# Order of the jobs beside attention, and the border of a local attention as one product, in a fused two-layer kernel on one Trainium2 core

## The chip, the cores and the metric

The kernel runs on one core of a Trainium2 chip. Its engines work side by side, each through its own list of instructions in order: TensorE (PE, matrix products), VectorE (DVE), ScalarE (ACT), GpSimd (POOL), and SyncE (SP), which here only issues transfers. They wait for each other by semaphores. The metric is the device time of one execution in microseconds (us), lower is better.

## The reference

Input and output are four images of 64 x 64 positions with 256 channels, float32. Two layers follow one another.

```python
# layer 0: attention over all 4096 positions of an image
q, k, v = x @ Wq + bq, x @ Wk + bk, x @ Wv + bv          # q, k: 32 channels
x = gamma * (softmax(q @ k.T) @ v) + x
# layer 1: 3x3 depthwise convolution to 3 x 256 channels, two pointwise layers, residual
hid = gelu(w_up1 @ conv3x3(x) + b_up1)                   # 768 -> 512 channels
h = x + (w_up2 @ hid + b_up2)                            # 512 -> 256
# then attention of each position over its 3x3 neighbours, padded with zeros, residual
q, k, v = split(w_qkv @ h + b_qkv)
w = softmax over the 9 neighbours of (q . k) / 16
out = h + sum over the 9 neighbours of w * v
```

At the border of an image the missing neighbours have k = b_k, so their scores are not zero weights: the kernel adds exp of a score for them to the denominator.

## The kernel before, in words

Everything is in one function, `unshifted`, with its order written out by hand. An image is cut into 8 blocks of 8 rows (512 positions); the four images give 32 **slots**. In a slot, layer 0 attends with the 512 queries of one block. A slot has 16 **points** (8 groups of keys, two halves each). At a point PE multiplies weights by values (`product`, L308, tile `acc`, eight records, 3.4 us); at every even point it first makes the next energies (`energy`, L289, tile `e`); ACT turns these into weights `p` (`weight`, L297); DVE sums them up (`add_up`, L322, tile `den`).

Layer 1 fills the gaps between these products, some slots later. The list `jobs` gives each point its pieces for block k = slot - 3 and block a = slot - 5. In order:

- `hidden_part` (L527): the first pointwise layer for half of the channels (d) in two parts, with 7 quarter products by recombined weights in place of 8. Part 0 makes `hid_a`, which ACT copies out (L540), and `hid_bc`, which DVE adds out (L534); part 1 makes `hid_de` and `hid_gf`, which DVE adds out, and ACT applies gelu (L550).
- `update` (L584, tile `dx`): the second pointwise layer; DVE adds the residual and stores `h` (L590).
- `guide` (L670, tile `g`, read out by ACT into `lq`) and `scores` (L763, tile `s`): the scores of the local attention, against `wg`, the product of the query and key weights. ACT takes exp (L783, tile `lp`), POOL masks the neighbours.
- `local_values` (L722, tile `lv`): values of half a block; DVE adds the bias (L735).
- `border`: `wc` times the pixels at the left and right edge, and of the first or last row of an image; a product with one output row (L702, tile `c`) of 8 and 8, and at 8 of the 32 blocks also 64, columns. ACT takes exp into `pad` (L708), POOL scales it.
- `local_sum` on POOL adds `lp` and `pad` to the denominator; `local_total` (tile `ld`) sums it over the partitions by a product with `ones`, `local_reciprocal` inverts it on DVE; `local_product` (L853, tile `lo`) makes the output, which DVE scales (L860), and one of POOL and DVE adds to `h`; SP sends it to memory.

The 3x3 convolution (`perceive`, L463) runs on DVE, whose generator `conv` is advanced by a number of **steps** at each point: a step is a tap (one instruction) or a recombination (L469); the first tap of each output is ACT's (L459). `n_steps` sets the pace, `-(-(point + 1) * n_steps // (points - 2))` steps up to each point.

At the end of a slot `partial_sums` and `finish` follow: DVE sums `den`, PE adds it up over the partitions (L361, tile `dps`), DVE inverts it, scales `acc` (L373) and adds the result into the ring of rows `xp` (L378); `rim` then copies or clears a border row of the ring. `finish` runs between the last point of a slot and point 0 of the next.

[...] four for `e`, two for `acc`, and two, tag `m`, that all jobs and `dps` take by turns (`job_bank`). A job's first product waits until the job two places before it has been read out of its bank.

The order of the work before, at the places which the change touches: point 0 holds `local_values` of block k-1 (second half), then part 0 of the hidden layer; `border` of block k-1 runs at point 8 ahead of the energies; in the last slot (31) the next block's jobs are put in as well and a second convolution is chained to the first (`upper`, all outputs without the last row's last taps). After slot 31 a tail without layer 0 finishes blocks 29 to 31, with jobs and convolution steps in a list of their own; it has four more banks. `DIRECT` is 28: blocks from there on have their output made in the tail. The tile `o` (two buffers) holds both the results of `finish` and the outputs `lo`.

Of the kernel before, what the change touches and what calls it, by code (L numbers as in the profile page):

```python
# [9 lines left out]
F32 = mybir.dt.float32  # L10
# [5 lines left out]
P = 128  # L16
# [4 lines left out]
HP, WP = H + 2, W + 2  # L21
NB = 512
RB = NB // W
NBLK = N // NB
NT = N // P
TPB = NB // P
# [25 lines left out]
def attention_then_perception_kernel(  # L52
# [34 lines left out]
    def unshifted():  # L87
# [54 lines left out]
        for c in range(CH):  # L142
            nc.gpsimd.memset(xp[:, c, 0:WP], 0.0)
            nc.gpsimd.memset(xp[:, c, (RP - 1) * WP :], 0.0)


        near = pool.tile([P, 2, QR, QW], F32, tag="near", name="near")
# [431 lines left out]
        def update(s, c):  # L579
            if c == 0:  # L580
                below(s)
            ps = job_bank(f"dx_{s}_{c}")
            for d in range(NHC):
                nc.tensor.matmul(  # L584
                    ps, lhsT=wup2[:, d, bass.ts(c, P)], rhs=hids[s][:, d, :],
                    start=(d == 0), stop=(d == NHC - 1),
                )
            for half in range(2):
                cols = slice(half * KW, (half + 1) * KW)
                nc.vector.scalar_tensor_tensor(  # L590
                    hs[s][:, c, half, HALO:, :],
                    ps.rearrange("p (h w) -> p h w", w=W)[:, :, cols],
                    bup2[:, c : c + 1],
                    xv[:, c, ring(s) : ring(s) + RB, 1 + cols.start : 1 + cols.stop],
                    ALU.add, ALU.add,
                )

# [85 lines left out]
        def edge_row(s):  # L685
            return {0: 0, NBLK - 1: RB - 1}.get(s % NBLK)

        def border(s):


            ps = job_bank(f"c_{s}")
            row = edge_row(s)
            n_side = 2 * RB
            parts = [
                (slice(half * RB, (half + 1) * RB), lambda h, half=half: h[:, :, half, half * (KW - 1)])
                for half in range(2)
            ]
            if row is not None:
                parts.append((slice(n_side, n_side + W), lambda h: h[:, row]))
            for to, of in parts:  # L700
                for kin in range(CH):
                    nc.tensor.matmul(  # L702
                        ps[0:1, to], lhsT=wc[:, kin : kin + 1], rhs=of(pixels(s, kin)),
                        start=(kin == 0), stop=(kin == CH - 1),
                    )
            n = parts[-1][0].stop
            one = pad[0:1, :]
            nc.scalar.activation(one[:, :n], ps[0:1, :n], AF.Exp, bias=bc, scale=-(C**-0.5))  # L708
            nc.gpsimd.tensor_scalar(one[:, :n], one[:, :n], 3.0, None, ALU.mult)
            if row is not None:  # L710

                ends = one[:, n_side : n : W - 1]
                nc.gpsimd.tensor_scalar(ends, ends, 2.0 / 3.0, None, ALU.mult)
# [133 lines left out]
        def local_product(s, c):  # L847
            b, g = divmod(s, NBLK)
            ps = job_bank(f"lo_{s}_{c}")
            pv = ps.rearrange("p (h w) -> p h w", w=W)  # L850
            todo = [(half, *piece) for half in range(2) for piece in pieces(s)]
            for i, (half, (block, t), rows, of) in enumerate(todo):
                nc.tensor.matmul(  # L853
                    pv[:, rows, columns(half)],
                    lhsT=lvs[block, t, half][:, bass.ts(c, P)],
                    rhs=near_ws[block, half][:, t, of, :],
                    start=(i == 0), stop=(i == len(todo) - 1), skip_group_check=True,
                )
            o = tile_of([P, NB], "o", f"lo_{s}_{c}", 2)
            nc.vector.tensor_tensor(o, ps, lrdens[s], ALU.mult)  # L860
            if s < NSLOT - 1:
                watch(o)
            engine, res = nc.gpsimd, o
            if s >= DIRECT and s != NSLOT - 2:

                if c == 0:
                    results[s] = tile_of([P, CH, NB], "xc", f"res_{s}", 2)
                engine, res = nc.vector, results[s][:, c, :]
            ov, rv = (t.rearrange("p (h a w) -> p h a w", a=2, w=KW) for t in (o, res))
            engine.tensor_tensor(rv, ov, pixels(s, c), ALU.add)  # L870
            nc.sync.dma_start(out=out[b, :, c, bass.ts(g, NB)], in_=res)
# [36 lines left out]
        for slot in range(NSLOT):  # L908
            b, g = divmod(slot, NBLK)
            if slot >= RING:  # L910
# [1 line left out]
            k, a = slot - LAG_HID, slot - LAG_ATT  # L912

            jobs = [
                job(local_values, k - 1, 1) + job(hidden_part, k, 0, 0),
                job(local_denominator, a) + job(hidden_part, k, 0, 1),
                job(hidden_part, k, 1, 0), job(hidden_part, k, 1, 1),
                job(local_product, a, 0), job(local_product, a, 1),
                job(update, k, 0), job(update, k, 1), [],
                job(guide, k, 0), job(guide, k, 1), job(scores, k, 0),  # L920
                job(scores, k, 1) + job(local_sum, k - 1), job(local_values, k, 0), [], [],
            ]
            if slot in (1, 2):
                jobs[0] = [lambda: next(combine)] * 2
# [10 lines left out]
            if slot == NSLOT - 1:  # L935


                jobs = [
                    job(local_values, k - 1, 1) + job(hidden_part, k, 0, 0),
                    job(local_denominator, a) + job(hidden_part, k, 0, 1),  # L940
                    job(hidden_part, k, 1, 0), job(hidden_part, k, 1, 1) + job(local_product, a, 0),
                    job(update, k, 0), job(update, k, 1) + job(local_product, a, 1),
                    job(local_values, k, 0) + job(guide, k, 0),
                    job(local_values, k, 1) + job(guide, k, 1),
                    job(scores, k, 0) + job(hidden_part, k + 1, 0, 0),
                    job(scores, k, 1) + job(local_sum, k - 1) + job(hidden_part, k + 1, 0, 1),
                    job(local_total, a + 1) + job(local_reciprocal, a + 1)
                    + job(hidden_part, k + 1, 1, 0),
                    job(hidden_part, k + 1, 1, 1), job(update, k + 1, 0) + job(border, k),
                    job(local_product, a + 1, 0) + job(update, k + 1, 1),  # L950
                    job(local_product, a + 1, 1) + job(local_values, k + 1, 0),
                    job(local_values, k + 1, 1),
                ]
                conv = chain(conv, perceive(slot - 1, upper))
                n_steps += NPC * (TAPS - 1 + 3)
            for point in range(points):
                G, half = divmod(point, 2)
                after = slot + (G + 1) // NG, (G + 1) % NG
                if half == 0:
                    if G == NG // 2 and slot + 1 < NSLOT:  # L960
                        spread_queries(slot + 1)

                    if G == NG // 2:
                        for do in job(border, k - 1):
                            do()
                    if after[0] < NSLOT:
                        energy(*after)
                if after[0] < NSLOT:
                    weight(*after, half)
                for do in jobs[point]:  # L970
                    do()
                product(slot, G, half)

                if point == 0:
                    add_up(slot, 0, 0)
                if point < points - 1:
                    add_up(slot, *divmod(point + 1, 2))
                else:
                    partial_sums(slot)

                to = min(n_steps, -(-(point + 1) * n_steps // (points - 2)))
                if point < 3:

                    to = min(to, n_mixed // MULT)
                while stepped < to:
                    next(conv, None)
                    stepped += 1
                if slot == 0 and point == NG:

                    next(combine)  # L990
                    blqk = loaded(b_lqk, "blqk")
                    wperc = loaded(w_perc, "wperc")
                    bperc = loaded(b_perc, "bperc")
                    wup1 = loaded(w_up1, "wup1")
                    bup1 = loaded(b_up1, "bup1")
                    wup2 = loaded(w_up2, "wup2")
                    mix_weights()
                    bup2 = loaded(b_up2, "bup2")
                    nc.sync.dma_start(out=wlv, in_=w_qkv[:, :, 2 * C :])
                    blv = loaded(b_lv.partition_broadcast(P), "blv", [P, C])  # L1000
                if nxt and half == 1:
                    for do in nxt[G]:
                        do()
                    if slot and G + 2 < NBLK:
                        fetch(slot + 1 + G + 2)
# [465 lines left out]
```

## Time and profile before

| | |
|---|---|
| time, median of three runs | 3551.79 us (3550.02 to 3551.85) |
| span of the profiled execution | 3549.7 us |
| PE busy | 98% of the span |
| DVE busy | 69% |
| ACT busy | 31% |
| POOL busy | 18% |
| granted PE clock, mean | 0.998 |
| slot, from the start of one to the next | 104.9 us |
| slot 31 (3282.7 to 3428.3) | 145.6 us |
| tail (3428.3 to the end) | 121.4 us |

Busy time is the time in which an engine has an instruction running. PE's records of one line are given with their count: a float32 product shows as two records. A wait is idle time of an engine put down to what released it; "issue" means that nothing in the profile was waited for. A line of a timeline gives the start in us from the start of the span, the length in us, the engine, the line of the kernel, the operation and the tiles (written <- read), and in brackets the idle time ahead of it with its releaser. The ends of PE's records are modelled, so the distance from one start to the next is the better measure of what PE work costs.

### The profile page before, as it was taken

The page shows a single profiled execution, that of the slowest core. Times are in us where ns is not written, and L with a number is a line of the kernel's source. Part 1 is how long each engine was busy: PE and PEld are TensorE (multiplying, and loading weights), DVE is VectorE, ACT ScalarE, POOL GpSimd, SP SyncE. Part 2 cuts the span into 40 slices and gives each one's busy share as a digit, 9 for nine tenths or more (in the row PEclk, how much of TensorE's full clock was granted, in tenths as well). Part 3 has the DMA queues.
Part 4 walks back from the last instruction along what each step waited for, and adds up shares of the span by engine and source line. Part 5 has one row for each costly group of instructions (what it writes and reads, how often), then busy time and mean ns, then how long its engine had stood idle before and what let it go on. Part 6 is the DMA issues. An engine that isn't in the chain of part 4 may idle for free.

```text
span 3549.7 us, 32536 instructions
## 1 busy us (share of the span) xinstructions
PE 3483.7 (98%) x12426; PEld 1903.1 (54%) x12426; DVE 2463.6 (69%) x3471; ACT 1084.7 (31%) x1336; POOL 628.9 (18%) x815
## 2 busy tenths in 40 slices
PE   9999999999999999999999999999999999999998
PEld 4444555555555555565555555555555555555555
DVE  1386777657777777765777777776577777777975
ACT  3232332323332323332332323333323323223331
POOL 2000012111121221121111212111121122121223
PEclk9999999999999999999999999999999999999999
DMA  3000000120000000011000000001100000000000
GB/s 104 7 4 10 7 16 19 24 48 16 9 16 7 16 15 15 22 27 42 15 16 16 4 13 16 15 22 36 33 15 16 16 10 10 13 15 16 7 6 25
DMA packets 92997, 66.86 MB, mean 19 GB/s; under 512 B 65856, under 2 KB 70976, under 8 KB 92704
## 3 DMA queue, kind: packets, MB, share of 16 engines
q1 hardware_dynamic: 92160, 64.29, 6.6%
q8 instruction: 100, 1.64, 0.2%
q14 instruction: 65, 0.53, 0.0%
q10 hardware_dynamic: 672, 0.39, 0.0%
HBM read 43.49 MB, written 18.81 MB: 18 GB/s over the span
## 4 chain that ended last, share of the span: by engine, by line
PE 92%; DVE 6%; issue 1%; DMA 0%; SPq 0%; POOL 0%; ACT 0%; ACTq 0%; DVEq 0%; POOLq 0%
PE acc L308 49%; PE e L289 7%; PE dx L584 6%; PE hid_bc L527 5%; PE hid_de L527 4%; PE hid_gf L527 4%; PE g L670 3%; PE v L255 3%; PE lo L853 3%; PE s L763 2%; PE lv L722 2%; DVE xp L378 1%; DVE perc L463 1%; PE hid_a L527 1%; PE hid L559 1%; PE qk L221 1%
## 5 line engine op out<-in xcount | busy, mean ns | idle before, releaser
L308 PE MATMUL acc<-p,v 128*128 128x512 f32 x4096 | 1842.4, 595 | 0.2 <-DVE o L373 0.2
L308 PEld LDWEIGHTS acc<-p,v 128*128 128x128 f32 x4096 | 765.7, 190 | 885.1 <-issue 876.2
L463 DVE SCALAR_TENSOR_TENSOR perc<-xp,wperc,perc 128x512 f32<-128x512 f32 (+2 forms) x1554 | 1159.3, 805 | 64.9 <-ACT perc L459 64.9
L297 ACT ACTIVATE p<-e 128x1024 f32<-128x1024 f32 x512 | 523.8, 1023 | 1473.9 <-PE e L289 471.0
L322 DVE TENSOR_TENSOR den<-den,p 128x1024 f32<-128x1024 f32 x480 | 586.1, 1221 | 104.0 <-ACT p L297 102.3
L181 POOL TENSOR_TENSOR watched<-watched,lo 128x256 f32<-128x256 f32 x124 | 150.0, 1210 | 1070.5 <-DVE lo L860 1065.5
L289 PE MATMUL e<-qa,ka 32*128 32x512 f32 x2048 | 292.0, 640 | 0.0
L584 PE MATMUL dx<-hid,wup 128*128 128x512 f32 x512 | 233.0, 598 | 0.0
L787 POOL TENSOR_TENSOR lp<-lp,near 128x396 f32<-128x396 f32 x60 | 87.2, 1453 | 678.3 <-ACT lp L783 678.3
L534 DVE TENSOR_TENSOR hid<-hid_bc,hid 128x512 f32<-128x512 f32 x60 | 41.5, 691 | 219.9 <-PE hid_bc L527 219.9
L735 DVE TENSOR_TENSOR lv<-lv,blv 128x256 f32<-128x256 f32 x126 | 47.1, 414 | 188.3 <-PE lv L722 188.3
L469 DVE TENSOR_TENSOR perc<-perc 128x256 f32<-128x256 f32 x360 | 171.6, 490 | 7.2
L527 PE MATMUL hid_de<-perc,wmix 128*128 128x256 f32 x720 | 165.2, 379 | 0.0
L584 PEld LDWEIGHTS dx<-hid,wup 128*128 128x128 f32 x512 | 94.7, 190 | 129.9 <-issue 101.4
L527 PEld LDWEIGHTS hid_de<-perc,wmix 128*128 128x128 f32 x720 | 136.8, 190 | 43.7 <-issue 28.2
L289 PEld LDWEIGHTS e<-qa,ka 32*128 32x128 f32 x2048 | 79.9, 183 | 148.0 <-issue 145.0
L550 ACT ACTIVATE hid<-hid,bup 128x512 f32<-128x512 f32 x120 | 80.1, 714 | 215.8 <-DVE hid L534 215.8
L459 ACT ACTIVATE perc<-xp,bperc,wperc 128x512 f32<-128x512 f32 x192 | 145.2, 806 | 0.0
L590 DVE SCALAR_TENSOR_TENSOR h<-dx,bup,xp 128x256 f32<-128x256 f32 x128 | 56.0, 479 | 117.9 <-PE dx L584 117.9
L527 PE MATMUL hid_bc<-perc,wup 128*128 128x256 f32 x360 | 90.5, 387 | 41.3 <-DVE lv L735 38.5
L722 PE MATMUL lv<-wlv,h 128*128 128x256 f32 x520 | 126.5, 385 | 3.9 <-DVE lv L735 3.1
L722 PEld LDWEIGHTS lv<-wlv,h 128*128 128x128 f32 x520 | 96.1, 190 | 53.8 <-issue 35.2
(143 smaller groups left out, 2907.3 us busy)
## 6 DMA issues: line engine op xcount, KB each, us to landing
xp<-in_x SPq DMA_DIRECT2D x30, 528.0 KB, 4.0
out<-lo SPq DMA_DIRECT2D x58, 256.0 KB, 2.0
xc<-in_x SPq DMA_DIRECT2D x56, 256.0 KB, 3.8
qa<-packed SPq DMA_DIRECT2D x124, 64.0 KB, 2.0
ka<-st SPq DMA_DIRECT2D x124, 16.0 KB, 1.8
packed<-st SPq DMA_DIRECT2D x31, 64.0 KB, 1.9
wup<-in_w_up SPq DMA_DIRECT2D x1, 1536.0 KB, 6.9
out<-res SPq DMA_DIRECT2D x6, 256.0 KB, 2.0
```

Of the source, the lines that this page charges most:

```text
L181: nc.gpsimd.tensor_tensor(at, at, values[:, i : min(n, i + C)], ALU.add)
L255: nc.tensor.matmul(ps[:, i * C : (i + 1) * C], lhsT=xc[:, kin, bass.ts(2 * pair + i, P)], rhs=wv[:, kin, :], start=(kin == 0), stop=(kin = ...
L289: nc.tensor.matmul(e[:, j, :], lhsT=key[rows, :], rhs=queries[s][rows, :], start=True, stop=True,)
L297: nc.scalar.activation(p, energies[s, G][:, 2 * half : 2 * half + 2, :], AF.Exp)
L308: nc.tensor.matmul(accs[s][c], lhsT=v[:, 2 * half + i, bass.ts(c, P)], rhs=p[:, i, :], start=(first and i == 0), stop=(G == NG - 1 and hal ...
L322: nc.vector.tensor_tensor(den, den, p, ALU.add)
L459: nc.scalar.activation(acc, win, AF.Identity, bias=bperc[:, half, j : j + 1], scale=wt)
L463: nc.vector.scalar_tensor_tensor(acc, win, wt, acc, ALU.mult, ALU.add)
L469: nc.vector.tensor_tensor(t[:, to, :], t[:, a, :], t[:, b, :], op)
L527: nc.tensor.matmul(ps[:, n * C : (n + 1) * C], lhsT=w(j), rhs=mixes[s, j][:, kind, :], start=(j == 0), stop=(j == MULT - 1),)
L584: nc.tensor.matmul(ps, lhsT=wup2[:, d, bass.ts(c, P)], rhs=hids[s][:, d, :], start=(d == 0), stop=(d == NHC - 1),)
L722: nc.tensor.matmul(ps[:, half * C : (half + 1) * C], lhsT=keys_of(s, t, half, kin), rhs=wlv[:, kin, :], start=(kin == 0), stop=(kin == CH ...
```

## The change

Six edits:

1. At point 0 of every slot part 0 of the hidden layer is put ahead of `local_values`; in slot 31 the guides go ahead of the local values too, and a hidden part ahead of `local_total` and `local_reciprocal`.
2. `border` is one product: DVE makes the sum over the two channel halves of `h` times `wc` in a tile `edge` (`border_terms`, two small instructions for each part, at the end of `update`), and PE multiplies it by `ones`, so that every partition gets the sum.
3. `border` moves from point 8 of the following slot to point 14 of the block's own slot.
4. In slot 31 `n_steps` counts 48 steps of the chained convolution, which is what it yields, in place of 66.
5. The outputs `lo` of blocks from 28 on use a buffer of `p` (three buffers, which hold weights until then) in place of one of `o` (two).
6. Ten products of `ones` by `ones` (128 columns) stand at the start of PE's list.

```diff
+WARM = 10
...
+        warm = bank("m", "warm")
+        for _ in range(WARM):
+            nc.tensor.matmul(warm[:, :P], lhsT=ones, rhs=ones, start=True, stop=True)
...
+            if c == CH - 1:
+                border_terms(s)
...
+        def border_terms(s):
+            for to, of in border_parts(s):
+                nc.vector.tensor_scalar(edge[:, to], of(0), wc[:, 0:1], None, ALU.mult)
+                nc.vector.scalar_tensor_tensor(
+                    edge[:, to], of(1), wc[:, 1:2], edge[:, to], ALU.mult, ALU.add
+                )
...
-            for to, of in parts:
-                for kin in range(CH):
-                    nc.tensor.matmul(
-                        ps[0:1, to], lhsT=wc[:, kin : kin + 1], rhs=of(pixels(s, kin)),
-                        start=(kin == 0), stop=(kin == CH - 1),
-                    )
-            n = parts[-1][0].stop
+            n = border_parts(s)[-1][0].stop
+            nc.tensor.matmul(ps[:, :n], lhsT=ones, rhs=edge[:, :n], start=True, stop=True)
...
-            o = tile_of([P, NB], "o", f"lo_{s}_{c}", 2)
+            if s < DIRECT:
+                o = tile_of([P, NB], "o", f"lo_{s}_{c}", 2)
+            else:
+                o = tile_of([P, 2, NB], "p", f"lo_{s}_{c}", 3)[:, 0, :]
...
-                job(local_values, k - 1, 1) + job(hidden_part, k, 0, 0),
+                job(hidden_part, k, 0, 0) + job(local_values, k - 1, 1),
...
-                job(scores, k, 1) + job(local_sum, k - 1), job(local_values, k, 0), [], [],
+                job(scores, k, 1) + job(local_sum, k - 1), job(local_values, k, 0), job(border, k), [],
...
-                    job(local_values, k, 0) + job(guide, k, 0),
-                    job(local_values, k, 1) + job(guide, k, 1),
+                    job(guide, k, 0) + job(local_values, k, 0),
+                    job(guide, k, 1) + job(local_values, k, 1),
...
-                    job(local_total, a + 1) + job(local_reciprocal, a + 1)
-                    + job(hidden_part, k + 1, 1, 0),
+                    job(hidden_part, k + 1, 1, 0) + job(local_total, a + 1)
+                    + job(local_reciprocal, a + 1),
...
-                n_steps += NPC * (TAPS - 1 + 3)
+                n_steps += NPC * (TAPS - 1)
...
-                    if G == NG // 2:
-                        for do in job(border, k - 1):
-                            do()
```

In `border_parts` the left edge has columns 0 to 7 of `edge`, the right edge 8 to 15, and an edge row, at the first and last block of an image, 16 to 79 in two halves of 32.

More of the change, by code (lines that the diff above doesn't have):

```diff
@@ L686, in edge_row, with border_parts @@
             return {0: 0, NBLK - 1: RB - 1}.get(s % NBLK)
+        edge = pool.tile([P, 2 * RB + W], F32, tag="edge", name="edge")
+        def border_parts(s):
+            row = edge_row(s)
+            parts = [
+                (slice(half * RB, (half + 1) * RB), lambda c, half=half: hs[s][:, c, half, HALO:, half * (KW - 1)])
+                for half in range(2)
+            ]
+            if row is not None:
+                parts += [
+                    (
+                        slice(2 * RB + half * KW, 2 * RB + (half + 1) * KW),
+                        lambda c, half=half: hs[s][:, c, half, HALO + row, :],
+                    )
+                    for half in range(2)
+                ]
+            return parts
+        def border_terms(s):
[3 more added lines that the diff above has]
+                    edge[:, to], of(1), wc[:, 1:2], edge[:, to], ALU.mult, ALU.add
+                )
         def border(s):
@@ L693, in border @@
             n_side = 2 * RB
[L694 to L699, printed above, removed]
-            for to, of in parts:
-                for kin in range(CH):
-                    nc.tensor.matmul(
-                        ps[0:1, to], lhsT=wc[:, kin : kin + 1], rhs=of(pixels(s, kin)),
-                        start=(kin == 0), stop=(kin == CH - 1),
-                    )
-            n = parts[-1][0].stop
+            n = border_parts(s)[-1][0].stop
+            nc.tensor.matmul(ps[:, :n], lhsT=ones, rhs=edge[:, :n], start=True, stop=True)
             one = pad[0:1, :]
@@ L938, in unshifted @@
                 jobs = [
-                    job(local_values, k - 1, 1) + job(hidden_part, k, 0, 0),
+                    job(hidden_part, k, 0, 0) + job(local_values, k - 1, 1),
                     job(local_denominator, a) + job(hidden_part, k, 0, 1),
```

## The prediction

> **What bounds the kernel now.** I read the page first, then the list of waits of TensorE (PE), then the timelines of PE, VectorE (DVE) and ScalarE (ACT) around one slot boundary, around the last slot and at both ends.
>
> ```profile
> PE 3483.7 (98%) x12426; PEld 1903.1 (54%) x12426; DVE 2463.6 (69%) x3471; ACT 1084.7 (31%) x1336; POOL 628.9 (18%) x815
> PE hid_bc L527 <- DVE lv L735: 38.5, 28, 1.4
> PE lv L722 <- DVE lv L735: 3.1, 1, 3.1
> PE hid_bc L527 <- DVE lturned L841: 2.8, 1, 2.8
> ```
>
> PE is busy all but 66 us of 3549.7, and the chain that ended last is 92% PE. So only two things can move the time: PE work, and the waits of PE (columns: total us, times, longest). One wait is 38.5 us: `hid_bc`, once in each of slots 4 to 31, for VectorE to empty a bank of local values. The boundary from slot 11 to 12 (start, us, what):
>
> ```profile
> 1324.36 0.30 PE L361 MATMUL dps<-parts,fold 128*128 128x32 f32 x2
> 1325.66 1.99 PE L722 MATMUL lv<-wlv,h 128*128 128x256 f32 x8
> 1327.49 1.46 PE L527 MATMUL hid_a<-perc,wup 128*128 128x256 f32 x6
> 1330.32 1.56 PE L527 MATMUL hid_bc<-perc,wup 128*128 128x256 f32 x6 [1.37 <-DVE lv L735]
> ...
> 1327.62 1.98 DVE L378 SCALAR_TENSOR_TENSOR xp<-o,gbv,xp 128x512 f32<-128x512 f32 x2
> 1329.52 0.74 DVE L735 TENSOR_TENSOR lv<-lv,blv 128x256 f32<-128x256 f32 x2
> ...
> 1329.63 0.30 ACT L399 COPY xp<-xp 128x132 f32<-128x132 f32 x1 [7.49 <-DVE xp L378]
> 1330.76 0.36 ACT L540 COPY hid<-hid_a 128x256 f32<-128x256 f32 x1
> 1433.82 0.37 ACT L540 COPY hid<-hid_a 128x256 f32<-128x256 f32 x1 [2.17 <-PE hid_a L527]
> ```
>
> Two banks alternate. `lv` is done at 1327.5, but DVE finishes the old slot until 1329.6 and only then empties it; `hid_bc` needs that bank. The last two lines matter later: in slot 12 ACT is held by the copy of a border row, in slot 13 it waits for PE.
>
> [...] eight `qk` matmuls take 3.04 us at 9.16 and 1.94 us at 18.00. [...] at 1329.63 everything on ACT stands behind the row copy.
>
> **The change part by part**, against the profiled span of 3549.7 (the timed runs, 3550.0 to 3551.9, have a median 2.1 higher; I take the saving off that).
>
> *Hidden quarters ahead of local values (slots 4 to 31).* New order: `dps`, energies, `hid_a`, `hid_bc`, `lv`. With `border` now just before `dps`, `hid_a` gets border's bank, `hid_bc` that of `dps` (emptied by the reciprocal at 1325.06), `lv` that of `hid_a` (emptied by the ACT copy). On the timeline: energies end and `hid_a` starts at 1325.66, takes 1.40; `hid_bc` starts at 1327.06 with no wait, takes 2.6; `lv` may start at 1329.66. Where ACT is free, as in slot 13, the copy follows `hid_a` within 0.5 us, long before: nothing waits, 1.37 is saved. DVE adds `hid_bc` at about 1330.0 and `lv` at 1331.6, while PE multiplies 3.4 us of `acc`; `hid_de` and `hid_gf` come later than both. Where ACT copies a border row (g = 3 and 4, four images, so 8 boundaries: the waits list has 4 + 4 of these, 7.5 us each) the copy of `hid_a` ends at 1331.12, `lv` waits 1.5, and the gain is nil. Sum: 20 x 1.37 = 27.4, and 8 x 0 = 0.
>
> *Border as one product.* Before, eight records take 0.28 us start to start, twelve 0.51:
>
> ```profile
> 1388.62 0.35 PE L702 MATMUL c<-h,small 128*1 128x8 f32 x8
> 3528.78 0.59 PE L702 MATMUL c<-h,small 128*1 128x8 f32 x12
> 3452.36 0.32 PE L833 MATMUL ld<-pad,ones 128*128 128x16 f32 x2
> ```
>
> (The next PE instructions start at 1388.90, 3529.29 and 3452.60.) After, one product of `ones` with 16 columns, the form of the third row: 0.24. For the 80 columns of the eight blocks at an image edge I take 0.25, since `dps` with 32 columns takes 0.23 (1324.36 to 1324.59). Saved: 24 x 0.04 + 8 x 0.26 = 3.0 us; bounds 0 (each product exposes 0.1 more behind the energies, as `acc` does: 3.70 there, 3.60 elsewhere) and 5 (it hides beside its neighbours).
>
> *Border terms on DVE.* Four small instructions more for each block, eight at an image edge. No row has their shape; nearest are scalar_tensor_tensor 128x1 (158 ns) and 128x64 (278 ns): 0.2 each, 0.8 us, or 1.6. In a slot they stand behind `h`; queued behind them are one `den` sum and the convolution's taps; DVE then idles 6.08 us before the next `lv` at 1417.8, so they cost 0, both bounds. In the tail DVE is full from 3461.8 to 3484.6 and `ld` waits 1.25 for a DVE mask: 0.6 lost there (0 to 1.5).
>
> *Border's new place.* Its exp on ACT follows the `p` exp of 1317.60, so about 1318.7. It overwrites `pad`, which POOL's `local_sum` reads until 1313.5: 5 us of room. Behind it on ACT is only the next `p`, at 1321.1. POOL's own small product follows into 7.7 us of idleness. No DMA is issued or passed. Cost 0.
>
> *Last slot.* The phantom steps go (126 to 108), so DVE takes 7.7 taps a point instead of 9, and 11 instead of 16 at point 3.
>
> ```profile
> 3320.51 12.63 DVE L463 SCALAR_TENSOR_TENSOR perc<-xp,wperc,perc 128x512 f32<-128x512 f32 x16
> 3342.39 8.01 DVE L463 SCALAR_TENSOR_TENSOR perc<-xp,wperc,perc 128x512 f32<-128x512 f32 x9
> 3351.12 1.99 PE L722 MATMUL lv<-wlv,h 128*128 128x256 f32 x8 [3.11 <-DVE lv L735]
> ```
>
> The reader sees bursts of taps on DVE, and PE stopped behind them. The waits of PE in this slot, beside that of `hid_bc` for `lv`, are 3.11 + 2.81 + 0.52 + 0.38 = 6.8 (the last two for `h`). With 11 taps (8.7 us) `h` is out at 3328 rather than 3334; guide ahead of `lv` puts 1.7 us more before the second `lv`, which needs its bank at about 3347 while DVE has emptied it by 3344; `ld` after the quarters is read by DVE 6 us before its bank is wanted. The tight place is point 8: step 60 of the mixed convolution now comes at point 7, about 3355, and `hid_bc` of the next block wants it at 3356. The work taken out of the middle lands in 11.7 us of DVE idleness after 3404. I take 6.0 (2 to 6.8).
>
> *The start.* Ten warm-up products of 128 columns fill PE from 1.05 (its operand is set by then) to 5.47, where it waits for `wv`. Twenty records of 99 columns go at 0.13 each in `lo` (twelve in 1.54)[...]: they end by 6.3, no later than the second `v` product, which waits for ACT's copy until 6.30 anyway. That costs 0. [...] six `v` records go in 1.3 instead of 2.2 us and the `qk` in 1.9 instead of 3.0. Those 2.0 pass on down the chain: ACT's `st`, its four transfers and its copies (the rows they copy have landed by 11.66), `qk` at 18.00, then SP's `ka` from 20.71, which SP reaches with 2 us to spare. I take 2.0; bounds 0 [...] and 2.6 (the restart of `qk` too).
>
> *The end.* `lo` of the last blocks takes three buffers `p` instead of two `o`.
>
> ```profile
> 3538.59 0.69 DVE L860 TENSOR_TENSOR lo<-lo,lrden 128x512 f32<-128x512 f32 x1 [0.73 <-DMA out<-lo]
> 3541.18 0.69 DVE L860 TENSOR_TENSOR lo<-lo,lrden 128x512 f32<-128x512 f32 x1 [1.18 <-DMA out<-lo]
> ```
>
> The first could start at 3537.87, the second after two 0.7 us operations, at 3539.3, when the buffer three back is free: 1.9 earlier, and nothing ends later than that chain.
>
> Sum: 27.4 + 3.0 + 6.0 + 2.0 + 1.9 - 0.6 = 39.7, rounded to 40: span 3510, time 3512.
>
> **Rivals.** *A, the wait moves to ACT in every slot*, not in eight: then 27.4 is lost and 12.6 remain, 3539. For it: [...] the row copies show what it does. Against: ACT L540 waited for PE, not the reverse, in 22 cases (44.5 us). *B, the last slot stays bound by DVE* (121.4 us busy of 145.6): the 6.0 becomes 0, and the start gives 0 too: 3520. For it: the margin of 1 us at point 8. Against: 11.7 us of idle DVE in that slot. *C, slower*: as A, but ACT later still. Price: the wait of `lv` is the end of ACT's copy less 1329.7, in 28 slots; it decides against the change from a wait of 1.37 + 12.6/28 = 1.8 us, so if every copy ends after 1331.5, 0.4 later than in the worst slots now. If it stood behind ACT's first taps (1.53 us) too, it would end at 1332.65: 28 x 1.6 - 12.6 = +32, 3584. Against: the taps come after the copy in the row order of ACT. *D, the order has no effect*: the bank is shared differently than I count and `hid_bc` still waits; then 12.6 as in A, or, with nothing else either, 3551.
>
> **How the numbers follow.** Likeliest 0.78 at 3512; B 0.10 at 3520; A with D's first form 0.07 at 3539; C 0.03; D with no effect 0.02. The low end adds the good bounds (2 + 0.8 + 0.6 + 0.6): 3508, less 3 for rim slots that gain a part: 3505. The high end takes B and the bad bounds of border and tail: 3524. A, C and D lie outside, 0.12. A measurement of this kernel tells 0.2% (7 us) from no change: faster 0.95, same 0.02, slower 0.03.
>
> **What would show it.** Right: the wait of `hid_bc` for `lv` gone from the list, 8 waits of `lv` for ACT L540 near 1.5 in its place; slots 103.5 apart instead of 104.9 except eight; two `c` records of 0.24; the last slot near 138 instead of 145.6; `qk` at about 16 instead of 18. Wrong: 28 waits of `lv` for ACT (A or C); a wait of `hid` quarters for `perc` in the last slot (B); longer stretches of PE at half clock than the 4.5 us after 3478.6, which no part of the sum foresees.

## The result, and the profile after

The changed kernel takes 3503.01 us (median of four, 3502.68 to 3504.98); the kernel before, beside it, 3551.69. The ratio is 0.9865, 95% interval 0.9848 to 0.9882. That is 48.7 us saved where 40 were forecast, and 2 us below the low end of the range.

The page after, busy times; then PE's waits (total us, times, longest):

```profile
PE 3476.9 (99%) x12222; PEld 1907.2 (54%) x12222; DVE 2497.1 (71%) x3631; ACT 1082.2 (31%) x1336; POOL 618.8 (18%) x815
```
```profile
PE lv L746 <- ACT hid L545: 11.2, 8, 1.7
PE good_sum L1094 <- DVE good L1090: 3.4, 1, 3.4
PE ld L857 <- DVE lp L811: 1.5, 1, 1.5
```

PE's busy time fell by 7 us only; the rest of the gain is waits that are gone. Of the 28 waits of `hid_bc` for `lv` none is left. In their place stand eight waits of `lv` for ACT.

The starts of `dps` cut the span into stages (so slot 31 of the kernel before is 145.8 here; cut at the energies that follow, it was 145.6). The forecast's sum is cut in the same way.

| stage | before | after | saved | forecast |
|---|---|---|---|---|
| start to the first `dps` | 114.6 | 111.6 | 3.0 | 2.0 |
| slots 1 to 30 | 3167.9 | 3134.0 | 33.9 | 28.7 |
| slot 31 | 145.8 | 136.0 | 9.8 | 7.4 |
| tail | 121.4 | 121.7 | -0.3 | 1.6 |
| span | 3549.7 | 3503.3 | 46.4 | 39.7 |

The profiled execution after is the slowest of its four, 2 us above the median, which is most of why the spans differ by 46.4 and the medians by 48.7.

An ordinary boundary, from slot 12 to 13, on PE's timeline. Before, the lines that matter are:

```profile
1429.42 1.14 PE L289 MATMUL e<-qa,ka 32*128 32x512 f32 x8
...
1432.32 1.46 PE L527 MATMUL hid_a<-perc,wup 128*128 128x256 f32 x6
1435.15 1.56 PE L527 MATMUL hid_bc<-perc,wup 128*128 128x256 f32 x6 [1.37 <-DVE lv L735]
...
1437.85 2.74 PE L308 MATMUL acc<-p,v 128*128 128x512 f32 x6
```

After:

```profile
1415.52 1.14 PE L294 MATMUL e<-qa,ka 32*128 32x512 f32 x8
1416.59 1.56 PE L532 MATMUL hid_a<-perc,wup 128*128 128x256 f32 x6
1417.99 1.46 PE L532 MATMUL hid_bc<-perc,wup 128*128 128x256 f32 x6
...
1420.58 1.89 PE L746 MATMUL lv<-wlv,h 128*128 128x256 f32 x8
1422.31 3.60 PE L313 MATMUL acc<-p,v 128*128 128x512 f32 x8
```

From `e` to `acc` it takes 8.43 before and 6.79 after: 1.64 saved, while the list of waits says 1.37. The difference has two parts. The record ahead of the wait is 1.46 long, but where nothing waits the next one starts 1.30 after it: the modelled end overhangs by 0.16, and idle time is counted only from there. And the first group after the wait takes 1.40 instead of 1.30 to the next start: 0.10 for starting again.

A boundary where ACT copies a border row, slot 11 to 12, PE and ACT:

```profile
1317.34 1.99 PE L746 MATMUL lv<-wlv,h 128*128 128x256 f32 x8 [1.37 <-ACT hid L545]
```
```profile
1315.80 0.30 ACT L404 COPY xp<-xp 128x132 f32<-128x132 f32 x1 [7.49 <-DVE xp L383]
1316.92 0.36 ACT L545 COPY hid<-hid_a 128x256 f32<-128x256 f32 x1
```

There the same loss has only changed its name, as forecast.

### The profile page after: what moved, and what is told of

Read it like the earlier page. It is cut to its first block, busy times and chain, and to the rows that moved or that the text cites. A ratio compares the mean times of both kernels' runs of the same rounds, so it can differ in the third digit from the quotient of the medians.

```text
span 3503.3 us, 32257 instructions
## 1 busy us (share of the span) xinstructions
PE 3476.9 (99%) x12222; PEld 1907.2 (54%) x12222; DVE 2497.1 (71%) x3631; ACT 1082.2 (31%) x1336; POOL 618.8 (18%) x815
## 4 chain that ended last, share of the span: by engine, by line
PE 98%; DVE 1%; ACT 0%; DMA 0%; SPq 0%; issue 0%; ACTq 0%; DVEq 0%
PE acc L313 50%; PE e L294 8%; PE dx L589 6%; PE hid_de L532 4%; PE hid_gf L532 4%; PE hid_bc L532 4%; PE g L677 3%; PE lv L746 3%; PE v L260 3%; PE lo L877 3%; PE s L787 3%; PE hid_a L532 3%; PE hid L564 1%; PE qk L226 1%; DVE perc L468 0%; PE c L730 0%
## 5 line engine op out<-in xcount | busy, mean ns | idle before, releaser
L186 POOL TENSOR_TENSOR watched<-watched,o 128x256 f32<-128x256 f32 x128 | 114.8, 897 | 56.0 <-DVE o L378 48.5
L677 PE MATMUL g<-h,wg 128*128 128x512 f32 x256 | 123.2, 604 | 0.0
```

What stands on the lines that cost most here:

```text
L186: nc.gpsimd.tensor_tensor(at, at, values[:, i : min(n, i + C)], ALU.add)
L677: nc.tensor.matmul(ps, lhsT=wg[:, kin, bass.ts(i, P)], rhs=pixels(s, kin), start=(kin == 0), stop=(kin == CH - 1),)
```

## The experiments

In the table, "ordinary" is the usual distance between `dps` in slots without a row copy on ACT, "row copy" in those with one. Middle is slots 1 to 30. All are from the one profiled execution of each; the ratio is of the timed runs to the kernel before on the same chip.

| kernel | ratio (95%) | to first dps | ordinary | row copy | middle | slot 31 | tail |
|---|---|---|---|---|---|---|---|
| before | 1 | 114.6 | 104.83 | 104.82 | 3167.9 | 145.8 | 121.4 |
| after | 0.9865 (0.9848 to 0.9882) | 111.6 | 103.13 | 104.77 | 3134.0 | 136.0 | 121.7 |
| order alone | 0.9912 (0.9897 to 0.9927) | 112.7 | 103.19 | 104.82 | 3136.7 | 146.8 | 121.3 |
| order back | 0.9960 (0.9946 to 0.9974) | 111.0 | 104.77 | 104.78 | 3165.2 | 137.7 | 120.1 |
| no warm-up | 0.9872 (0.9857 to 0.9888) | 112.3 | 103.13 | 104.76 | 3134.0 | 136.0 | 119.5 |
| steps back | 0.9882 (0.9867 to 0.9897) | 111.3 | 103.14 | 104.77 | 3134.0 | 141.4 | 121.8 |
| last order back | 0.9865 (0.9850 to 0.9880) | 111.7 | 103.14 | 104.76 | 3134.0 | 138.3 | 119.3 |
| old border form | 0.9869 (0.9854 to 0.9884) | 111.1 | 103.19 | 104.83 | 3137.2 | 136.3 | 118.9 |
| buffers o | 0.9866 (0.9851 to 0.9881) | 111.7 | 103.13 | 104.77 | 3134.0 | 136.0 | 121.4 |
| row copies on POOL | 0.9822 (0.9809 to 0.9836) | 110.8 | 103.13 | 103.14 | 3120.6 | 136.0 | 120.0 |
| the same, tail's border old | 0.9828 (0.9814 to 0.9841) | 111.2 | 103.13 | 103.14 | 3120.6 | 136.0 | 119.5 |
| ACT held in every slot | 0.9955 (0.9940 to 0.9970) | 111.0 | 104.76 | 104.77 | 3165.0 | 137.7 | 120.0 |

**Order alone** and **order back**: the two edits are

```diff
-                job(local_values, k - 1, 1) + job(hidden_part, k, 0, 0),
+                job(hidden_part, k, 0, 0) + job(local_values, k - 1, 1),
```

in both lists of jobs of the kernel before, and the reverse in the changed one.

> The kernel before with one edit, the hidden quarters ahead of the local values at point 0. Theory 1 (a wait in the list costs its idle time plus 0.26 us: 0.16 by which the modelled end of the last record overhangs the next start, and 0.10 for the restart of PE): 1.63 us in each of 20 ordinary slots, 32.6 us faster than before, ordinary slots 103.2 apart, eight slots unchanged. Theory 2 (the wait costs what the list says, 1.37, and the missing gain is that of the border): 27.4 us faster, ordinary slots 103.46 apart.

> The changed kernel with the old order at point 0 alone. Theory 1: the 28 waits of hid_bc for lv come back, the eight of lv for ACT go, 32.6 us slower than the changed kernel, about 14 to 16 us faster than before. Theory 2: 27.4 us slower than the changed kernel, 20 us faster than before.

Measured: alone 3518.89 against 3549.62 (30.7 faster), back 3535.65 on the same chip. In the middle, which holds 19 of the 20 ordinary slots, the order is worth 3167.9 - 3136.7 = 31.2 in one direction and 3165.2 - 3134.0 = 31.2 in the other, so 1.64 a slot. Theory 1 holds; 1.37 would have given 26. The whole of order alone falls short of 32.6 for a reason of its own in slot 31, shown in the last section. With the old order the waits are these:

```profile
PE hid_bc L532 <- DVE lv L759: 38.7, 28, 1.7
```

**No warm-up**: the ten products and their bank are taken out.

```diff
-        for _ in range(WARM):
-            nc.tensor.matmul(warm[:, :P], lhsT=ones, rhs=ones, start=True, stop=True)
```

> The changed kernel without the ten warm-up products. If they act as worked out, by warm v and qk records alone: 2.0 to 2.3 us slower than the changed kernel, qk at 18.0 instead of 15.7. If the transfers behind it move too: 3.0 slower at the first dps (114.6 instead of 111.6). Rival, that they do nothing for the end since a transfer sets the start: 0.

Measured: 3504.21, at a ratio that the interval doesn't tell from the changed kernel's. PE's timeline without, and then with, the warm-up:

```profile
5.29 3.73 PE L257 MATMUL v<-wv,xc 128*128 128x256 f32 x8 [5.29 <-DMA wv<-in_w_v]
8.95 1.94 PE L223 MATMUL qk<-xc,wqk 128*64 128x512 f32 x8
```
```profile
1.07 4.51 PE L149 MATMUL warm<-ones 128*128 128x128 f32 x20 [1.07 <-POOL ones L141]
5.77 2.27 PE L260 MATMUL v<-wv,xc 128*128 128x256 f32 x8 [0.20 <-DMA wv<-in_w_v]
7.97 1.94 PE L226 MATMUL qk<-xc,wqk 128*64 128x512 f32 x8
```

The twenty records end by 5.6, before the 6.3 that the forecast counted. `v` goes faster, 2.27 against 3.73. But in this execution without warm-up `qk` took 1.94 at 8.95, where the kernel before, with the same work ahead of it, took 3.04 at 9.16: how fast PE goes by then was not the same in these two executions. Here 1.0 is gained at `qk` and 0.7 at the first `dps`. Over all profiles the first `dps` comes at 112.3 to 114.6 without (three, mean 113.2) and at 110.8 to 111.7 with warm-up (nine, mean 111.3). So it is worth about 1.9 us on the mean, within the bounds, though three executions are few; the 3.0 of the table holds a slow start of the one execution before.

**Steps back** and **last order back** take the two edits of slot 31 apart.

```diff
-                n_steps += NPC * (TAPS - 1)
+                n_steps += NPC * (TAPS - 1 + 3)
```

> The changed kernel with the 66 steps counted in the last slot instead of 48, so DVE's bursts as before, in the new order of the jobs. Theory P (the pace sets the waits of the last slot): waits of PE for DVE of 3 to 7 us come back in that slot, which takes 139 to 143 instead of 136.0. Theory O (the order of the jobs does it): no more than 1 us comes back.

```diff
-                    job(guide, k, 0) + job(local_values, k, 0),
-                    job(guide, k, 1) + job(local_values, k, 1),
+                    job(local_values, k, 0) + job(guide, k, 0),
+                    job(local_values, k, 1) + job(guide, k, 1),
...
-                    job(hidden_part, k + 1, 1, 0) + job(local_total, a + 1)
-                    + job(local_reciprocal, a + 1),
+                    job(local_total, a + 1) + job(local_reciprocal, a + 1)
+                    + job(hidden_part, k + 1, 1, 0),
```

> The changed kernel with the jobs of points 6, 7 and 10 of the last slot in the old order (local values ahead of guides, local total ahead of the hidden part), at the new pace of 48 steps. If the pace did most of it (putting it back alone gave 141.4 for the slot): 137 to 139 us for the slot, with the wait of hid_bc for lturned back at 1 to 3 us. If order and pace each give their part and add up: 140.4, since the slot was 144.2 without both.

Measured: the slot is 5.4 us longer with the old pace (141.4) and 2.3 with the old order (138.3). With the pace back, PE's timeline of that slot shows these waits; the last line is a stretch of it (columns: stretch, its length, PE busy with the number of records, granted clock, DMA share, GB/s):

```profile
3295.20 1.77 PE L877 MATMUL lo<-lp,lv 128*128 128x99 f32 x12 [0.39 <-DVE h L595]
3302.02 1.96 PE L677 MATMUL g<-h,wg 128*128 128x512 f32 x4 [0.52 <-DVE edge L718]
3313.05 2.56 PE L746 MATMUL lv<-wlv,h 128*128 128x256 f32 x8 [2.19 <-DVE lv L759]
```
```profile
3314.34:3317.75 3.41, 3.41 (x7) 0.50 0.00 0
```

The listed waits are 3.1 us, the slot is 5.4 longer. From start to start the waits cost 3.7; the other 1.7 is PE at half clock (granted clock 0.50) for 3.41 us after the wait of 2.19 (`lv` takes 2.56, where the changed kernel has 1.89). This execution is the slowest of its four, 3.4 above the fastest. With the order back the waits are 1.2 of `hid_bc` for `lturned` and 0.5 of `lv`, and nothing in the slot runs at half clock (`lv` takes 1.99 and 2.00, `g` 1.88).

So without the clock the pace alone is worth 3.7 and the order alone 2.3, together 6.0. Before, with both in the old form, the four waits of this slot cost 7.6 from start to start, and none was followed by half clock (granted clock 1.00 over the slot). The parts do not simply add up: some 1.6 us of the waits come only when pace and order are both old. That 5.4 + 2.3 also makes 7.7 is chance, by the half clock of one execution. The 138.3 fits the 137 to 139 expected if the pace did most, not the 140.4 expected of parts that add up. Theory P has the larger share.

**Old border form** at the new place, without the DVE terms.

```diff
-            if c == CH - 1:
-                border_terms(s)
...
-            nc.tensor.matmul(ps[:, :n], lhsT=ones, rhs=edge[:, :n], start=True, stop=True)
...
+            for to, of in parts:
+                for kin in range(CH):
+                    nc.tensor.matmul(ps[0:1, to], lhsT=wc[:, kin : kin + 1], rhs=of(pixels(s, kin)), ...)
```

> The changed kernel with border as four or six small products at its new place, and without the DVE terms. By the step of the prediction (0.04 us a block, 0.26 at an image edge) the slots 1 to 30 get 2.7 us longer, 27 blocks of them. By the rival that it is the place that counted and not the form: 0. In the tail the waits of ld for DVE fall from 1.8 to 1.25 and the tail gets 0.5 to 1.1 shorter: about 2 us slower in all.

Measured: the middle 3.2 longer, the tail 2.8 shorter, 0.9869 in all. The middle agrees with the step (28 blocks by the forecast's terms: 2.7). Most of the tail's 2.8 is the clock: the changed kernel's execution had 6.83 us at half clock there, this one none ahead of the last `lo` (mean granted clock of the tail 0.95 and 0.98; last section). Beside the two tails of the new form that also had none (119.5 without warm-up, 119.4 with the last order back), the old form's 118.9 is 0.5 to 0.6 shorter: so much the DVE terms cost there, less what the one product saves. `ld` waits 1.2 + 0.2 for DVE with the old form, 1.5 + 0.5 with the new. The two instructions of the terms have medians of 225 and 227 ns in the changed kernel, near the estimate of 0.2.

**Buffers o** for the last outputs:

```diff
-            if s < DIRECT:
-                o = tile_of([P, NB], "o", f"lo_{s}_{c}", 2)
-            else:
-                o = tile_of([P, 2, NB], "p", f"lo_{s}_{c}", 3)[:, 0, :]
+            o = tile_of([P, NB], "o", f"lo_{s}_{c}", 2)
```

> The changed kernel with the two buffers o for the outputs of blocks 28 to 31. If the chain at the end is what it was: the two lo of the last block wait for transfers again and the end, from the last PE product of lo, is 1.4 to 1.9 us later. If the tail's later PE work has taken the slack: 0.5 or less.

Measured: from the last `lo` group on PE to the end it takes 11.7 with `o` and 10.0 in the changed kernel: 1.7. By the tails it is 1.9 to 2.0: 121.4 against the 119.5 and 119.4 of the two other executions without half clock there (16 records of `hid` take 7.41 with `o`, as with the last order back). The timed runs (3504.91) don't show it apart. With `o` the last two `lo` wait 0.45 and 1.44 for transfers; in the changed kernel they stand without a wait:

```profile
3493.27 0.69 DVE L887 TENSOR_TENSOR lo<-lo,lrden 128x512 f32<-128x512 f32 x1
3494.83 0.68 DVE L887 TENSOR_TENSOR lo<-lo,lrden 128x512 f32<-128x512 f32 x1
```

**Row copies on POOL** and **ACT held in every slot** test what makes the eight slow slots, once by taking the cause away and once by putting it everywhere.

```diff
-                nc.scalar.copy(xv[:, :, 0, :], xv[:, :, RP - 2, :])
+                nc.gpsimd.tensor_copy(xv[:, :, 0, :], xv[:, :, RP - 2, :])
...
-                nc.scalar.copy(xv[:, :, RP - 1, :], xv[:, :, 1, :])
+                nc.gpsimd.tensor_copy(xv[:, :, RP - 1, :], xv[:, :, 1, :])
```

> The changed kernel with the two copies of a border row of the ring made by POOL, not by ACT. If ACT, held by that copy, is what keeps the eight slots at 104.8: the eight waits of lv for ACT go, those slots are 103.1 apart, 8 x 1.63 = 13.0 us faster than the changed kernel. Rival, that the copy on POOL comes late for the convolution or holds the watch sums and with them the buffers: a new wait for POOL, gain below 5 us.

```diff
+            if g not in (RING - 1, RING):
+                held = tile_of([P, CH, W], "held", f"held_{s}")
+                nc.scalar.copy(held, xv[:, :, ring(s) + RB - 1, 1 : 1 + W])
```

> The changed kernel with one more copy on ACT in each ordinary slot, of the rows that finish has just written, into a tile that nobody reads: ACT is then held in every slot as in the eight. If the order of ACT's queue makes the wait of lv: 28 waits of lv for ACT, every slot 104.8 apart, 20 x 1.63 = 32.6 us slower than the changed kernel. If those eight slots are slow for another reason of the ring's border rows: ordinary slots stay at 103.1.

Measured: with POOL the eight waits are gone and every slot takes 103.13, the middle is 13.4 us shorter, the time 3489.26 against 3552.11. With ACT held, all slots take 104.8 and the list of waits reads

```profile
PE lv L749 <- ACT hid L548: 38.5, 28, 1.7
```

with the time at 3535.2: rival A of the prediction, made real (its 3539 was 3535 here). So one copy of 0.3 us, at the head of ACT's queue and waiting for DVE, is worth 1.64 us of PE in each of those slots. On POOL the copy shows no cost: the engine had been waiting for DVE anyway, and only watch sums stand behind it.

```profile
1309.46 0.29 POOL L404 COPY xp<-xp 128x132 f32<-128x132 f32 x1 [3.48 <-DVE xp L383]
1309.71 3.14 POOL L186 TENSOR_TENSOR watched<-watched,o 128x256 f32<-128x256 f32 x4
```

This version beats both kernels: its interval (0.9809 to 0.9836) lies below that of the changed kernel (0.9848 to 0.9882).

**The same, with the tail's border in its old form** for blocks 30 and 31:

```diff
-            if c == CH - 1:
+            if c == CH - 1 and s < NSLOT - 3 + 1:
                 border_terms(s)
...
+            if s >= NSLOT - 3 + 1:
...
+                for to, of in parts:
+                    for kin in range(CH):
+                        nc.tensor.matmul(
+                            ps[0:1, to], lhsT=wc[:, kin : kin + 1], rhs=of(pixels(s, kin)),
+                            start=(kin == 0), stop=(kin == CH - 1),
+                        )
+            else:
+                nc.tensor.matmul(ps[:, :n], lhsT=ones, rhs=edge[:, :n], start=True, stop=True)
```

> The changed kernel with the row copies on POOL and, for the blocks 30 and 31 of the tail alone, border in its old form of small products and without DVE terms. If the DVE terms in the tail are what delays ld there: its waits fall from 1.8 to 1.25 and the tail, 120.0 with the copies on POOL alone, takes 118.5 to 119.5; ratio to the kernel before 0.981 to 0.982. If the length of the tail is set by the clock that PE is granted there: 118.5 to 121.5, no clear gain over 0.9822.

Measured: 3490.05, ratio 0.9828, not told from the version above. The waits of `ld` did fall to 1.2 + 0.2, and the tail from 120.0 to 119.5. Both tails had 3.41 us at half clock (mean granted clock 0.96 in both; the 24 records of `hid` take 12.24 and 12.26 without a stop), so the 0.5 is the form's, as above. But 119.5 lies inside what both statements allowed, and the timed runs show no gain: no reason to keep two forms.

## Why the prediction was right or wrong

**Direction, mechanism and place** were right: the bank traffic at point 0, no wait in ordinary slots, the same loss under ACT's name in eight slots, nothing new elsewhere.

**What failed is the size of the first term**, "nothing waits, 1.37 is saved", and by the same fault that of the last slot. I took the price of a wait from the list of waits. It is 1.64 from start to start: 20 x 0.27 = 5.4 us more. Both numbers stood in the timeline that the prediction used: 8.42 from the energies at 1324.59 to `acc` at 1333.01, against 6.8 by adding the groups' own distances. My walk through the new order had the right start of `lv`, 1329.66, and was not carried on to `acc`, which then comes at 1331.4, 1.6 earlier than before.

**The last slot**, 6.0 of the 6.8 listed, fell short too: from start to start the four waits of before were 3.38, 3.06, 0.59 and 0.55, which is 7.6. I had cut the listed 6.8 for the tight place at point 8, and no wait came up there: after the change PE waits for nothing in this slot. The 9.8 saved in slot 31 are these 7.6, the 1.64 at point 0, and about 0.6 that were not taken apart.

With these two terms at their measured size the sum is 39.7 + 5.4 + 1.6 = 46.7, and the time 3505. That the spans differ by 46.4 is in part luck: the start gained 1.0 more than forecast and slot 31 another 0.5, while the tail gained 1.9 less. The 2 us from 3505 to the median of 3503 belong to no part of the sum that was found; the forecast set one profiled execution against a median.

**Border as one product**: 3.0 forecast for all blocks, 3.2 measured in the middle. Right. **DVE terms**: 0 in the slots, right; in the tail 0.6 forecast, 0.6 more waiting seen, and tails 0.5 to 0.6 longer. **Border's new place**: no new wait of PE is listed for ACT or POOL there; right. **The start**: 2.0, and 1.9 between the means of the profiles. **The buffers**: 1.9, measured 1.7 to 2.0. **The tail as a whole** shows no gain in the one execution after, because PE ran at half clock there for 6.83 us, and for 3.41 before (last section). Set beside the tails after the change that also had 3.41 (120.0: row copies on POOL, ACT held), the 121.4 of before is 1.4 longer, where 1.6 was forecast. The prediction named longer stretches at half clock as outside its sum; the one that it read as 4.5 us is 3.4 by the granted clock.

**Rivals.** A and C didn't come about, and ACT held in every slot shows that the mechanism was real. B is refuted: the last slot gave more than its term. D is refuted by the order alone.

## What to carry to other kernels

Price a wait of PE by the distance from the start before it to the start after it, against the same groups where nothing waits; a list of idle times starts at a modelled end and leaves out the restart (0.16 and 0.10 us here, so 1.64 for a listed 1.37). When two banks go round between engines, write down who empties each bank for the new order, and look for the one cheap instruction that holds that engine's queue for something unrelated: moving it to an idle engine gained here what eight reordered slots had not. Compare stages only between executions with the same granted clock in them (here the tail took 119.5 without and 121.7 with 6.83 us at half clock). Pace filler work by what its generator yields, because surplus counts turn into bursts ahead of evictions (66 steps counted in place of 48 cost slot 31 3.7 us here, the half clock not counted).

## What the runs showed of the hardware that was not expected

In slot 31 some waits of PE of 2 to 3 us were followed by 3.41 us at half clock (granted clock 0.50), which cost 1.7 us beside the wait: after 2.19 with the steps back, after 3.11 and 2.02 with the order alone. The first of order alone:

```profile
3316.40 2.48 PE L722 MATMUL lv<-wlv,h 128*128 128x256 f32 x8 [3.11 <-DVE lv L735]
3318.68 3.13 PE L670 MATMUL g<-h,wg 128*128 128x512 f32 x4
```

`g` takes 3.13 instead of 1.88, `lv` 2.48 instead of 1.99; after its wait of 2.02 at `hid_bc` the same happens again (granted clock 0.72 over 3350 to 3356, as over 3316 to 3322). That is 3.4 us, and it explains why this slot took 146.8 there though a wait was gone. In the kernel before, the same wait of 3.11 at the same place left `g` at 1.88.

These are two stretches of 3.41 us around the wait of 3.11, first in order alone, then in the kernel before (columns as above):

```profile
3314.35:3317.76 3.41, 1.36 (x6) 1.00 0.00 0
3317.76:3321.17 3.41, 3.41 (x6) 0.50 0.00 0
```
```profile
3346.23:3349.64 3.41, 1.77 (x5) 1.00 0.20 77
3349.64:3353.05 3.41, 1.93 (x9) 1.00 0.00 0
```

In order alone the stretch that ends where the half clock begins has PE busy for 1.36 us. In the kernel before the two stretches have 1.77 and 1.93 us, and the clock stays at 1.00. What makes the clock fall after one wait and not after the other was not shown: no run tested it.

In the tail, where PE makes small products with waits of 1.2 to 1.5 us between them, the same is seen in some executions. The stretches are of the changed kernel and of the one without warm-up:

```profile
3432.28:3439.11 6.83, 6.72 (x13) 0.50 0.00 0
```
```profile
3429.03:3442.00 12.97, 10.39 (x36) 1.00 0.00 1
```

There too the runs do not show what decides it. But the length of the tail follows the clock. With the border terms on DVE and the buffers `p`, tails are 119.4 to 119.5 long with no half clock in them ahead of the last `lo` products (no warm-up, with 1.00 in the stretch above; last order back, with a mean of 0.98 over the tail), 120.0 with 3.41 us of it (row copies on POOL, ACT held; mean 0.96) and 121.7 with 6.83 us (the changed kernel; mean 0.95). Some half clock comes behind the last `lo` as well: the mean from 3494.0 to the end is 0.67 in the changed kernel. Which execution is hit could not be tied to an edit.
